# Layer 1's attention scores: from two products of 512 columns in two row groups to four of 256 columns in four row groups

## The chip, the cores and the metric

One Trainium2 chip; the kernel runs on 1 of its cores. The metric is the device time of one execution in microseconds (us), the median of several executions. The engines are TensorE (in the profile PE for its products and PEld for its weight loads), VectorE (DVE), ScalarE (ACT), GpSimd (POOL) and SyncE (SP, which here only issues transfers). Products are written to PSUM[...].

## The reference

Eight batches of 128 tokens of width 512 pass through four layers. Each layer is a cross-attention and then a feed-forward part, both added to the running `x`, which is normalised before each part:

```python
x = x + _L0_xattn_ref(_layernorm(x), ...)   # 32 heads of 128
x = x + _L0_ffn_ref(_layernorm(x), ...)     # base product and gated low-rank experts
x = x + _L1_xattn_ref(_layernorm(x), ctx_4096, mask, ...)
x = x + _L1_ffn_ref(_layernorm(x), ...)     # int8 product
x = x + _L2_xattn_ref(...)                  # 32 query heads, 8 key heads, rotary
x = x + _L2_ffn_ref(...)                    # weights rounded to NF4 and back
x = x + _L3_xattn_ref(...)
x = x + _L3_ffn_ref(...)
```

The change touches the attention of layer 1 only:

```python
def _L1_xattn_ref(qk, v, masks, Wq, bq, Wk, bk, Wv, bv, Wo, bo):
    W, H, D, DK = 128, 8, 128, 64
    # each batch's 128 x 512 is cut into 4 patches of 128 x 128
    q = einsum('ed,bdw->bew', Wq, qp) + bq[:, None]      # 64 rows: 8 heads of 8
    k = einsum('ed,bdw->bew', Wk, qp) + bk[:, None]
    val = einsum('ed,bdw->bew', Wv, vp) + bv[:, None]
    scores = einsum('bhdi,bhdj->bhij', qh, kh) / sqrt(8)
    scores = where(mask > 0, scores, -1e9)
    attn = softmax(scores)
    o = einsum('bhij,bhdj->bhdi', attn, vh)
    o = gelu(o)
    out = (einsum('de,bew->bdw', Wo, o) + bo[:, None]) * masks
```

A head has only 8 rows. For one patch of one batch there are eight score matrices of 128 x 128.

## The kernel before

All tensors are float32 unless a line says otherwise. The work is one long, unrolled program. Its backbone is a list of 128 units: a unit is one attention head for one half of the batches (four batches), first of layer 0 (`Unit0`, 64 units) and then of layer 2 (`Unit2`, 64 units). A unit projects keys and queries, makes scores three units ahead or two, turns the softmax's output through DRAM, weighs the values (L297), and every fourth unit adds a group's output to `x` (L218).

Everything shorter is put into *slots* between a unit's pieces. `slot()` calls what a table has written for the current slot number, and then works off some pieces of the NF4 rounding of layer 2's feed-forward weights. `short_stages(hf)` fills that table for one half: the feed-forward part of layer 0 (`F0`), layer 1's attention (`L1`), layer 1's feed-forward part (`F1`). So layer 1's attention for batches 0 to 3 runs while `Unit0` units of the second half are the main work, and for batches 4 to 7 while `Unit2` units of the first half are.

Within `L1`, batch i of a half starts at slot t = 18 + 13 i. `norm` runs at t - 1 and `project` at t: one product (L516) gives queries on partitions 0 to 63 and keys on 64 to 127, ScalarE adds the bias (L518) into `qk`, and VectorE makes four masked copies of the keys (L521) in `km`, in each of which only the rows of two of the eight heads are not zero. The 64 rows of keys are two strips of 32, and each strip holds four heads; so one product of a strip of queries with that strip's four masked copies gives the scores of four heads side by side. `score(b, n)` runs at t + 2, 5, 8 and 11, one patch each time: two products of 32 rows and 512 columns (L540) into two PSUM tiles; VectorE reads each, scales it and adds the mask (L542), then takes the maximum (L544); ScalarE takes the exponentials (L213); the result is scaled (L548), transposed in blocks (L240) and sent through DRAM by POOL's queue (L242, L245). `project_values` runs at t + 7 (product L527, read by VectorE at L529). `weigh(b, n)` runs at t + 9, 12, 15 and 18 (product L557 in four column groups, read by ScalarE at L558), `close` and `output` at t + 18 and t + 19. Where the batches' ranges overlap, a slot has a `score` of one batch and then a `weigh` of the one before: slots 33, 36, 46, 49, 59 and 62.

PSUM tiles come from two streams. The main stream has two banks for products, and one each for turns (`tp`), scores and weighed values; the units' own work uses it. The side stream rotates three banks for everything in the slots:

```python
main = Main("m", None, ps, {"mm": ("mm", 2), "tp": ("tp", 1), "sc": ("sc", 1), "pv": ("pv", 1)})
side = Stream("s", sub_pool("side", 2), ps, {k: ("side", 3) for k in ("mm", "tp", "sc", "pv", "po")})
```

So a new side tile waits until the one taken three tiles earlier has been read. Main's `tp` bank serves the first three units and the loading of the first contexts; after that a unit's turn goes through DRAM and main takes no `tp` tile while the side stream runs.

The framework that builds the program draws all waits itself. It also sets the order of each engine's instructions ahead of time, from the order of the calls and its own estimate of when each is ready.

Of the kernel before, what the change touches and what calls it, by code (L numbers as in the profile page):

```python
# [11 lines left out]
F32 = mybir.dt.float32  # L12
# [5 lines left out]
AF = mybir.ActivationFunctionType  # L18
ALU = mybir.AluOpType
# [4 lines left out]
P = 128  # L24
B = 8
D = 512
# [36 lines left out]
def kernel(ctx: ExitStack, tc: tile.TileContext, a, out):  # L63
    nc = tc.nc
    V, S, G, T = nc.vector, nc.scalar, nc.gpsimd, nc.tensor
# [15 lines left out]
    class Stream:  # L81


        def __init__(self, name, sb, ps, banks):
            self.name, self.sb, self.ps, self.banks = name, sb, ps, banks
# [46 lines left out]
    def along(v, n):  # L132

        return v.unsqueeze(2).to_broadcast([v.shape[0], v.shape[1], n])

    def times(v, n):

        return v.unsqueeze(1).to_broadcast([v.shape[0], n, v.shape[1]])
# [70 lines left out]
    def exps(dst, src, su, n, negm, scale=None):  # L209

        for h in range(n):
            by = 1.0 if scale is None else scale[:, h:h + 1]
            S.activation(dst(h), src(h), AF.Exp, bias=negm[:, h:h + 1], scale=by, accum_out=su[:, h:h + 1])  # L213
# [19 lines left out]
    def blocks_turned(pool_, src, name, bufs, queue=nc.sync):  # L233

        h, n = src.shape[1], src.shape[2] // P
        tb = pool_.tile([P, 4 * n, h, 32], F32, tag="tb" + name, name="tb", bufs=bufs[0])
        V.transpose(tb, src.rearrange("p h (c k) -> p c h k", k=32))  # L240
        far = dram.tile([4, 32, n, 4, 32 * h], F32, tag="far" + name, name="far", bufs=4)
        queue.dma_start(far.rearrange("a i s b n -> (a i) (s b n)"), tb.rearrange("p c h j -> p (c h j)"))  # L242
        pt = pool_.tile([P, n, 4, h, 32], F32, tag="pt" + name, name="pt", bufs=bufs[1])
        for b in range(4):
            queue.dma_start(pt[32 * b:32 * b + 32].rearrange("p s a h j -> p s a (h j)"), far[:, :, :, b, :].rearrange("a i s n -> i s a n"))  # L245
        return pt

    def project(st, w, xT):

        mm = st.mm()  # L250
        for c in range(DC):
            T.matmul(mm, lhsT=w[:, c, :], rhs=xT[:, c, :], start=c == 0, stop=c == DC - 1)  # L252
        return mm
# [90 lines left out]
    class Unit0(Unit):  # L344
        def project_k(self):
            st, g, grp = self.st, self.g, self.group
            if self.h == 0:
                grp.bias = ap_.tile([P, 4, P], F32, tag="rot", name="bias")
                load(grp.bias, a["l0_bias"][g])
            self.k = tile_of("k", 3)  # L350
            S.copy(self.k, project(st, of_head(a["l0_wk"][g], self.h), ctxT[:, :, self.hf * 512:(self.hf + 1) * 512]))

        def project_q(self):
            st, g, grp = self.st, self.g, self.group
            self.q = tile_of("q", 3)
            S.copy(self.q, project(st, of_head(a["l0_wq"][g], self.h), xT0[self.hf]))
            if self.h == 0:
                self.load_values()
            if self.h == 3:
                grp.wo = by_chunk(a["l0_wo"][g])  # L360
# [8 lines left out]
        def score(self):  # L369
            s = self.score_tile()  # L370
            mark[0] = V.tensor_add(s, self.scores(self.k), times(self.group.bias[:, self.h, :], HALF))
            V.tensor_add(s, s, neg0[:, self.hf * HALF:(self.hf + 1) * HALF, :])
            self.softmax(s)
            V.tensor_mul(self.su, self.su, anyv[:, self.hf * HALF:(self.hf + 1) * HALF])
            V.tensor_mul(s, s, along(self.su, P))
# [99 lines left out]

    class L1:
        def __init__(self, st, hf):
            self.st, self.hf = st, hf  # L480
# [33 lines left out]
        def project(self, b):  # L514
            mm = self.st.mm()
            T.matmul(mm, lhsT=self.wqk[:, 0:2, :].rearrange("p s d -> p (s d)"), rhs=self.h, start=True, stop=True)  # L516
            self.qk = self.l1.tile([P, D], F32, tag="qk1", name="qk1", bufs=1)
            S.activation(self.qk, mm, AF.Identity, bias=self.bqk)  # L518
            self.km = self.l1.tile([64, 4, D], F32, tag="km", name="km", bufs=1)
            for hd in range(4):  # L520
                V.tensor_scalar(self.km[:, hd, :], self.qk[64:128, :], self.h4[64:128, hd:hd + 1], None, ALU.mult)  # L521

        def project_values(self, b):
            mm = self.st.mm()
# [9 lines left out]
        def score(self, b, n):  # L534
            st, w = self.st, slice(n * P, (n + 1) * P)
            s = self.l1.tile([P, 8, P], F32, tag="s1", name="s1", bufs=1)
            scs = [st.sc() for j in range(2)]
            for j in range(2):
                r = slice(32 * j, 32 * (j + 1))
                T.matmul(scs[j], lhsT=self.qk[r, w], rhs=self.km[r, :, w], start=True, stop=True)  # L540
            for j in range(2):
                V.scalar_tensor_tensor(s[:, 4 * j:4 * j + 4, :], scs[j], 1.0 / math.sqrt(8.0), times(self.neg[:, w], 4), ALU.mult, ALU.add)  # L542
            mx = st.small(8, "mx")
            V.tensor_reduce(mx, s, AX.X, ALU.max, negate=True)  # L544
            su = st.small(8, "su8")
            exps(lambda h: s[:, h, :], lambda h: s[:, h, :], su, 8, mx)
            V.reciprocal(su, su)
            V.tensor_mul(s, s, along(su, P))  # L548
            self.pts[n] = blocks_turned(self.l1, s, "1", (1, 2), G)[:, 0]
# [115 lines left out]
    class Unit2(Unit):  # L665
# [20 lines left out]
        def project_q(self):  # L686
            self.q = tile_of("q", 3)
            rope(self.q, project(self.st, of_head(a["l2_wq"][self.g], self.h), xT2[self.hf]), cs[self.hf])
            if self.h == 3:
                self.group.wo = by_chunk(a["l2_wo"][self.g])  # L690
# [411 lines left out]
    with ExitStack() as early:  # L1102
        def sub_pool(name, bufs, **kw):
            return early.enter_context(tc.tile_pool(name=name, bufs=bufs, **kw))
# [10 lines left out]
        main = Main("m", None, ps, {"mm": ("mm", 2), "tp": ("tp", 1), "sc": ("sc", 1), "pv": ("pv", 1)})  # L1115
        side = Stream("s", sub_pool("side", 2), ps, {k: ("side", 3) for k in ("mm", "tp", "sc", "pv", "po")})


        NF4_PACE = ((2.1, 2.1), (0.9, 2.2), (0.2, 1.6), (1.6, 1.6))
        xT0, xT2 = [], []  # L1120
# [343 lines left out]
def build(arrays):  # L1464
    import concourse.bacc as bacc

    nc = bacc.Bacc("TRN2", target_bir_lowering=False, num_devices=1)
    aps = {
        n: nc.dram_tensor(f"in_{n}", v.shape, mybir.dt.from_np(v.dtype), kind="ExternalInput").ap()
        for n, v in arrays.items()  # L1470
    }
    out = nc.dram_tensor("out_0", (B, P, D), F32, kind="ExternalOutput").ap()
    with tile.TileContext(nc) as tc:
        kernel(tc, aps, out)
    return nc
# [9 lines left out]
```

## Time and profile before

| what | us |
|---|---|
| median of 3 executions | 3075.28 (3073.91 to 3076.26) |
| the profiled execution's own time | 3075.35 |
| span of its records | 3073.6 |
| TensorE products in flight | 3041.6 |
| VectorE busy | 1876.2 |
| ScalarE busy | 1373.3 |
| POOL busy | 384.4 |

The span is 1.75 us shorter than the time of the same execution. A row of a line's group gives count, then shortest, median and longest duration in ns, then first and last start. A row of the timeline gives start and duration in us, engine, line, operation, the tiles written and read, the shape, how many neighbours were merged, and in brackets how long the engine had been idle and what released it. A float32 product shows as two records, each of which is a pass over all its columns; a record's duration is from its start until its last result is out, so neighbours overlap: full-height passes of 512 columns start 0.429 us apart and last 0.59. "PE busy" therefore means that a product is in flight. Transfers keep the 16 DMA engines under half busy (37.3% for the largest queue).

### The profile page before, as it was taken

The page shows a single profiled execution, that of the slowest core. Times are in us where ns is not written, and L with a number is a line of the kernel's source. Part 1 is how long each engine was busy: PE and PEld are TensorE (multiplying, and loading weights), DVE is VectorE, ACT ScalarE, POOL GpSimd, SP SyncE. Part 2 cuts the span into 40 slices and gives each one's busy share as a digit, 9 for nine tenths or more (in the row PEclk, how much of TensorE's full clock was granted, in tenths as well). Part 3 has the DMA queues.
Part 4 walks back from the last instruction along what each step waited for, and adds up shares of the span by engine and source line. Part 5 has one row for each costly group of instructions (what it writes and reads, how often), then busy time and mean ns, then how long its engine had stood idle before and what let it go on. Part 6 is the DMA issues. An engine that isn't in the chain of part 4 may idle for free.

```text
span 3073.6 us, 35109 instructions
## 1 busy us (share of the span) xinstructions
PE 3041.6 (99%) x10720; PEld 1668.8 (54%) x10724; DVE 1876.2 (61%) x3765; ACT 1373.3 (45%) x3856; POOL 384.4 (13%) x490
## 2 busy tenths in 40 slices
PE   9999999999999999999999999999999999999999
PEld 4555555544444565555555554445656656555554
DVE  5666666657766566898889862214554555555544
ACT  4555555435654433665556641003343433433332
POOL 2000000101211021332111110001111111111110
PEclk9999999999999999999999999999999999999999
DMA  6434343336654533665344342223565645655540
GB/s 216 127 113 120 120 134 116 110 100 181 177 157 126 153 111 92 179 188 171 117 139 129 122 121 77 78 73 117 165 193 165 193 161 176 189 173 168 175 126 14
DMA packets 425564, 427.42 MB, mean 139 GB/s; under 512 B 40160, under 2 KB 315296, under 8 KB 424864
## 3 DMA queue, kind: packets, MB, share of 16 engines
q1 hardware_dynamic: 391200, 348.60, 37.3%
q10 hardware_dynamic: 23040, 41.95, 4.4%
q0 software_dynamic: 11136, 34.61, 3.8%
q8 instruction: 87, 1.43, 0.2%
q14 instruction: 101, 0.83, 0.1%
HBM read 308.70 MB, written 116.33 MB: 138 GB/s over the span
## 4 chain that ended last, share of the span: by engine, by line
PE 47%; DVE 3%; ACT 1%; issue 0%; POOL 0%; DVEq 0%; ACTq 0%; POOLq 0%
PE po L218 7%; PE tp L945 7%; PE mm L968 7%; PE mm L903 5%; PE mm L218 4%; PE pv L1028 4%; PE sc L1005 3%; PE mm L252 3%; PE mm L912 2%; PE mm L1096 1%; PE mm L1084 1%; PE pv L297 1%; DVE dq L750 1%; PE sc L280 1%; PE mm L682 1%; PE mm L672 1%
## 5 line engine op out<-in xcount | busy, mean ns | idle before, releaser
L252 PE MATMUL mm<-xT,w 128*128 128x512 f32 x1024 | 466.0, 597 | 2.3 <-DVE rot L662 2.3
L218 PE MATMUL mm<-w,o 128*128 128x512 f32 x1024 | 465.1, 598 | 1.6 <-ACT o L299 1.5
L739 ACT ACTIVATE ind<-nw,bounds 128x512 f32<-128x512 f32 (+2 forms) x510 | 350.0, 703 | 235.5 <-DVE dq L750 162.8
L750 DVE SCALAR_TENSOR_TENSOR dq<-ind,dq 128x512 f32<-128x512 f32 (+2 forms) x476 | 333.1, 700 | 23.0 <-ACT ind L739 8.2
L252 PEld LDWEIGHTS mm<-xT,w 128*128 128x128 f32 x1024 | 190.1, 191 | 220.5 <-issue 211.7
L218 PEld LDWEIGHTS mm<-w,o 128*128 128x128 f32 x1024 | 189.7, 191 | 220.4 <-issue 208.5
L213 ACT ACTIVATE s<-s,nm 128x128 f32<-128x128 f32 x512 | 198.3, 388 | 101.9 <-DVE nm L271 101.2
L968 PE MATMUL mm<-w,xT 128*128 128x512 f32 x512 | 233.9, 592 | 0.0
L218 PE MATMUL po<-w,o 128*128 128x512 f32 x512 | 233.2, 594 | 0.0
L252 PE MATMUL mm<-ctxT,w 128*128 128x512 f32 x512 | 230.4, 593 | 0.8 <-ACT ctxT L1249 0.8
L384 PE MATMUL mm<-w,ctxT 128*128 128x512 f32 x512 | 230.4, 593 | 0.0
L213 ACT ACTIVATE p<-sc,nm,rq 128x256 f32<-128x256 f32 x256 | 141.1, 562 | 114.6 <-DVE nm L1010 110.9
L219 DVE TENSOR_TENSOR x<-x,mm 128x512 f32<-128x512 f32 x128 | 87.1, 680 | 143.1 <-PE mm L218 142.8
L280 PEld LDWEIGHTS sc<-k,q 128*128 128x128 f32 x1024 | 131.7, 192 | 49.8 <-issue 44.6
L159 POOL TENSOR_TENSOR rs<-rs,mhalf 128x1 f32<-128x1 f32 x64 | 38.2, 598 | 950.6 <-DVE rs L180 510.0
L218 PEld LDWEIGHTS po<-w,o 128*128 128x128 f32 x512 | 96.3, 190 | 110.6 <-issue 102.8
L384 PEld LDWEIGHTS mm<-w,ctxT 128*128 128x128 f32 x512 | 94.7, 190 | 108.0 <-issue 107.1
L903 PE MATMUL mm<-xT,w 128*128 128x512 f32 (+1 forms) x352 | 152.5, 592 | 0.8 <-DVE x L219 0.8
L299 ACT COPY o<-pv 128x512 f32<-128x512 f32 x128 | 74.3, 580 | 173.8 <-PE pv L297 173.7
L1009 DVE TENSOR_REDUCE nm<-sc 128x2 f32<-128x512 f32 x128 | 85.3, 674 | 103.1 <-PE sc L1005 102.8
L252 PEld LDWEIGHTS mm<-ctxT,w 128*128 128x128 f32 x512 | 93.4, 190 | 99.1 <-issue 97.8
L968 PEld LDWEIGHTS mm<-w,xT 128*128 128x128 f32 x512 | 97.0, 190 | 89.4 <-issue 84.7
(254 smaller groups left out, 4749.0 us busy)
## 6 DMA issues: line engine op xcount, KB each, us to landing
w<-in_l_wq SPq DMA_DIRECT2D x128, 256.0 KB
w<-in_l_wo SPq DMA_DIRECT2D x128, 256.0 KB
far<-tb SPq DMA_DIRECT2D x125, 256.0 KB
pt<-far SPq DMA_DIRECT2D x500, 64.0 KB
far<-tb SPq DMA_DIRECT2D x60, 512.0 KB
pt<-far SPq DMA_DIRECT2D x240, 128.0 KB
far<-tb SPq DMA_DIRECT2D x63, 384.0 KB
pt<-far SPq DMA_DIRECT2D x252, 96.0 KB
```

Source lines behind the costliest of these rows:

```text
L213: S.activation(dst(h), src(h), AF.Exp, bias=negm[:, h:h + 1], scale=by, accum_out=su[:, h:h + 1])
L218: T.matmul(mm, lhsT=o(h), rhs=wo[h], start=h == 0, stop=h == 3)
L252: T.matmul(mm, lhsT=w[:, c, :], rhs=xT[:, c, :], start=c == 0, stop=c == DC - 1)
L280: T.matmul(sc[:, i, :], lhsT=self.q[:, i * P:(i + 1) * P], rhs=k[:, i * P:(i + 1) * P], start=True, stop=True)
L384: T.matmul(mm, lhsT=ctxT[:, c, toks(self.hf * HALF + i)], rhs=grp.wv[c], start=c == 0, stop=c == DC - 1)
L739: S.activation(ind, w, AF.Relu, bias=bounds[:n, i:i + 1], scale=(down + up)[i][1])
L750: V.scalar_tensor_tensor(dst, ind, step, dst, ALU.min, ALU.subtract if i == len(down) else ALU.add)
L903: T.matmul(mm[:n, :], lhsT=w[c][:, j * P:j * P + n], rhs=xT[:, c, :], start=c == 0, stop=c == DC - 1)
L945: T.matmul(it.kv[:, s, :], lhsT=lhsT, rhs=it.wkv[c // 2][:, c % 2, :], start=c == 0, stop=c == DC - 1)
L968: T.matmul(mq, lhsT=self.xT[it.hf][:, c, cols(it.b)], rhs=it.wq[c], start=c == 0, stop=c == DC - 1)
L1005: T.matmul(sc[:, i, :], lhsT=it.qT[2 * j + i], rhs=it.kT, start=True, stop=True)
L1028: T.matmul(pv, lhsT=it.v[:, j, :], rhs=it.pts[j], start=j == 0, stop=j == 1)
```

## The change

`project` keeps a second copy of the queries on partitions 64 to 127 (`again`, made by ScalarE), and `km` holds the four masked key copies as two on partitions 0 to 63 and two on 64 to 127. `score` makes four products of 32 rows and 256 columns, each in a row group of its own (partitions 0, 32, 64, 96), each into a PSUM tile of its own. Three of these come from the side stream's three banks, the fourth from the bank of main's `tp`. VectorE reads each of the four with an instruction of its own, and the pairs of heads go to the places they had before.

```diff
@@ project
-            self.qk = self.l1.tile([P, D], F32, tag="qk1", name="qk1", bufs=1)
-            S.activation(self.qk, mm, AF.Identity, bias=self.bqk)
-            self.km = self.l1.tile([64, 4, D], F32, tag="km", name="km", bufs=1)
+            qk = self.l1.tile([P, D], F32, tag="qk1", name="qk1", bufs=1)
+            S.activation(qk, mm, AF.Identity, bias=self.bqk)
+            again = self.l1.tile([P, D], F32, tag="q1", name="q1", bufs=1)
+            S.copy(again[64:128, :], qk[0:64, :])
+            self.q = [qk, qk, again, again]
+            self.km = self.l1.tile([P, 2, D], F32, tag="km", name="km", bufs=1)
             for hd in range(4):
-                V.tensor_scalar(self.km[:, hd, :], self.qk[64:128, :], self.h4[64:128, hd:hd + 1], None, ALU.mult)
+                r = 64 * (hd // 2)
+                V.tensor_scalar(self.km[r:r + 64, hd % 2, :], qk[64:128, :], self.h4[64:128, hd:hd + 1], None, ALU.mult)
@@ score
-            scs = [st.sc() for j in range(2)]
-            for j in range(2):
+            scs = [st.psum(kind, (P, 2, P)) for kind in ("sc", "sc", "sc", "sc4")]
+            for j, sc in enumerate(scs):
                 r = slice(32 * j, 32 * (j + 1))
-                T.matmul(scs[j], lhsT=self.qk[r, w], rhs=self.km[r, :, w], start=True, stop=True)
-            for j in range(2):
-                V.scalar_tensor_tensor(s[:, 4 * j:4 * j + 4, :], scs[j], 1.0 / math.sqrt(8.0), times(self.neg[:, w], 4), ALU.mult, ALU.add)
+                T.matmul(sc, lhsT=self.q[j][r, w], rhs=self.km[r, :, w], start=True, stop=True)
+            for sc, h in zip(scs, (0, 4, 2, 6)):
+                V.scalar_tensor_tensor(s[:, h:h + 2, :], sc, 1.0 / math.sqrt(8.0), times(self.neg[:, w], 2), ALU.mult, ALU.add)
@@ the streams
         side = Stream("s", sub_pool("side", 2), ps, {k: ("side", 3) for k in ("mm", "tp", "sc", "pv", "po")})
+
+        side.banks["sc4"] = ("tp", 1)
```

## The prediction

> **What bounds the kernel now.** I read the page's busy times first, then the stretches of layer 1, the lines of its scores, and two short timelines around single scores.
>
> The page, rows of the whole execution:
>
> ```profile
> span 3073.6 us, 35109 instructions
> PE 3041.6 (99%) x10720; PEld 1668.8 (54%) x10724; DVE 1876.2 (61%) x3765; ACT 1373.3 (45%) x3856; POOL 384.4 (13%) x490
> ```
>
> TensorE is busy or has a product in flight all the time, so time taken off it should come off the end, unless a wait takes its place. Busy times of the two stretches in which layer 1's scores run (first and second half of the batches; columns PE, PEld, DVE, ACT, POOL, then granted clock):
>
> ```profile
> 667.00:878.00 211.00, 211.00 (x843) 102.40 (x843) 161.57 (x278) 122.53 (x415) 40.10 (x72) 1.00 0.60 169
> 1199.00:1406.00 207.00, 198.81 (x950) 107.38 (x950) 183.76 (x292) 125.55 (x491) 66.54 (x92) 0.98 0.58 172
> ```
>
> They differ. In the first TensorE never idles and VectorE has slack (162 of 211 us). In the second VectorE is at 184 of 207 us and TensorE already loses 8 us. What the score products and their readers cost, from the two lines' own rows:
>
> ```profile
> L540 PE MATMUL sc<-km,qk x128: 587/625/692, 667.0 to 1394.6; 32*128 32x512 f32 x128
> L542 DVE SCALAR_TENSOR_TENSOR s<-sc,neg x64: 646/681/693, 668.6 to 1405.5; 128x512 f32<-128x512 f32 x64
> ```
>
> 128 records are 64 products, two records each: 32 scores of two products. One score of the first half, in order of time (start, duration, engine):
>
> ```profile
> 723.90 1.13 PE L540 MATMUL sc<-km,qk 32*128 32x512 f32 x4
> 724.96 0.64 PE L557 MATMUL pv<-pt,vt 128*32 128x128 f32 x16
> 725.06 1.29 DVE L542 SCALAR_TENSOR_TENSOR s<-sc,neg 128x512 f32<-128x512 f32 x2 [3.43 <-PE sc L540]
> ```
>
> Four records in 1.13 us, where four of a full-height 512-column product stand 0.43 us apart: the two row groups already run side by side. And the `weigh` product (L557) starts 1.06 us after the score, before VectorE has touched the score: it has a bank of its own. In the second half the reader comes late:
>
> ```profile
> 1224.37 1.00 PE L527 MATMUL mm<-wqk,h 128*128 128x64 f32 x8
> 1225.30 1.43 PE L540 MATMUL sc<-km,qk 32*128 32x512 f32 x4
> 1226.66 4.56 PE L218 MATMUL mm<-w,o 128*128 128x512 f32 x10
> ...
> 1234.10 0.28 DVE L529 TENSOR_TENSOR vt<-mm,bv 128x128 f32<-128x128 f32 x1
> ...
> 1236.09 1.27 DVE L542 SCALAR_TENSOR_TENSOR s<-sc,neg 128x512 f32<-128x512 f32 x2
> ```
>
> The value projection (L527) is read at last at 1234.10, the score of 1225.30 from 1236.09. VectorE trails by some 9 us here, and only free banks let TensorE go on.
>
> **The products: a gain of 13.2 us.** Between neighbouring records (single instructions of the timeline) a score's first pass starts at 723.899, the second at 724.432 (0.533 later), the next work at 724.956 (0.525 later). Full-height records stand 0.429 apart, so 0.427 of each is the stream of 512 columns and about 0.1 is loading and changing the array's shape. With 256 columns the stream halves to 0.2135: 0.320 + 0.312, and two more row groups start 0.0066 later each, as the two do now: 0.645 instead of 1.058 us. 0.413 x 32 scores = 13.2 us of TensorE, if four row groups run at once as two do. Near row: L557 runs four column groups with starts 0.006 apart, 16 records in 0.57 us. Bounds: nothing saved if the groups go two by two; no more than 13.2.
>
> **VectorE: +4.5 to +9.5 us, partly hidden.** Two reads of 128x512 (681 ns) become four of 128x256. The row for that width is L837, SBUF to SBUF, 418 ns: 4 x 0.418 - 2 x 0.681 = 0.31 us a score, 9.9 in all; back to back they overlap (starts 0.604 apart for 0.69), which makes it 0.14, or 4.5. I take 4.5. In the first half the slack covers it; in the second, half of it (2 us) can reach TensorE. Without cover it is the whole 4.5 to 9.9. The key masks (L521, 486 ns, four a batch) stay as many on as many partitions: nothing.
>
> **ScalarE: +4.6 us, hidden.** One copy of 64x512 a batch, 8 x 0.57 (copies of that width, L351 and L356). It runs behind L518 beside VectorE's four masks (1.7 us), and the batch's first score comes 6 us or more after L518; ScalarE is busy 123 and 126 us in the two stretches. Behind it wait the exponentials, by 0.57 us eight times. If nothing covered it: 4.6. No DMA is added or moved, so the queues of SP and POOL get nothing; POOL issues the turned scores when VectorE has them, later by the 0.14.
>
> **The banks: +4 and +4 us, the doubtful part.** The side stream rotates three banks. A score took two, now it takes all three, and the unused turn bank of the main stream. Two waits are new.
>
> First, `weigh` in the same slot as a score, 12 of 32 times (slots 33, 36, 46, 49, 59, 62 of each half), had the third bank; now it needs the score's first bank, free when the first quarter is read. Score end (0.72) + 0.41 of reading + about 0.09 of semaphores = 1.22 us after the score's start, where TensorE is ready at 0.645: 0.58 us each with VectorE at hand. VectorE's lag at these twelve, by the readers' starts: 0.03, 0.49, 0.03, 0.03, 0.19, 0.03 in the first half; 0, 1.35, 0.56, 1.10, 0.81, 1.99 in the second. Taken in order that is 7.0 for the twelve and 6.2 of lags: 13.2 us, all of the gain. But the framework orders each engine ahead of time by readiness (L297 of this unit stands at 1231.06, behind the outputs written after it), so it can put a main product between. Then a lone `weigh` costs 0.20 more: score and `weigh` together take 1.83 us out of the stream, apart 1.255 + 0.772. That is 2.4 for twelve. Between 2.4 and 13.2 I take 4, as in the first half the reader is nearly always at hand.
>
> Second, a score that follows a value projection needs that projection's bank. In the first half VectorE has read it in time. In the second, three scores (1225.30, 1282.86, 1386.30) would wait for 1234.38, 1287.88 and 1389.90: 9 + 5 + 3.6 = 17.6 us if nothing is put between. The outputs (L218, 4.6 us right behind the first) and other products can be, and an earlier stall lets VectorE catch up, so later ones (2.5 and 1.3 us before L540 already) shrink. Between 0 and 17.6 I take 4.
>
> Queued behind a waiting score on TensorE is all of the main attention work, and VectorE and ScalarE behind that.
>
> **A rule against the change.** The row: a score's readers need 1.29 us now and 1.43 after, its products 1.06 now and 0.645 after. The Trainium skill's "TensorEngine Tiling (Array Packing)", section "PSUM Bottleneck", says in substance that tiling quickens TensorE and not the emptying of PSUM, which can become the limit; "Gotcha 1: PSUM Pressure" adds that row tiles need different banks. By the rule alone each bank is held at VectorE's pace, the in-order price stands (13.2 + 17.6), and the sum is +18. By the trace the reader is at hand in the first half and there is other work for TensorE, and the sum is negative. No run here shows four row groups. I go by the trace for the first half and between the two for the second.
>
> **Sum.** -13.2 + 4 + 4 = -5.2, the 2 us of VectorE being inside the second 4. The profiled execution took 3075.35 us (span 3073.6 and 1.75 around it), 0.07 from the median 3075.28: 3075.35 - 5.2 = 3070.
>
> **Rivals.**
> - *Nearly all kept.* The ordering fills every wait; only the 2.4 for lone `weigh`s is paid: -10.8, 3064.5. For: no idle TensorE in the first half. Against: in the second, stalls at L540 (2.5 and 1.3 us) show an order that did not foresee VectorE.
> - *The banks decide: slower.* In the second half scores and `weigh`s wait for VectorE in the written order: 17.6 + 9.3 there, less 6.6 of gain, some 5 of relief and 5 of the first half's net gain: about +10, 3085. Place: L540 and L557 from 1199 to 1406. It decides once the waits exceed 13.2 us, 0.9 us for each of the fifteen products named. For: lags of 4 to 10 us there. Against: the planner's reordering seen above.
> - *No fourfold row groups.* The products go two by two: no gain, the 8 of waits stay, and each pair's own loading (0.1 x 2 x 32 = 6) is paid: +14, 3089. Against: four column groups do run together.
>
> **How the numbers follow.** Forecast (3065 to 3076) 0.36, nearly all kept 0.24, banks decide 0.34, no fourfold groups 0.06. 0.2% is 6.15 us, about what a measurement of this kernel can tell from no change. Faster (under 3069.1): 0.15 of the forecast and 0.23 of the second, 0.38. Slower (over 3081.4): 0.26 of the banks, 0.05 of the last, and 0.01 of reordering far behind the change: 0.32. The same: 0.30. The range runs from 3061 (nearly all kept, a little relief on top) to 3090 (the two slower cases); the likeliest case alone is 3065 to 3076.
>
> **What would show it.** The score's group: 256 records of 32x256, eight in 0.65 to 0.75 us for each score; over 1.0 and the fourfold groups fail. VectorE's reads x128 near 0.41 us. `weigh` moved away from the score by one main product, or TensorE idle before L557 on a releaser L542. Idle TensorE before L540 between 1199 and 1406: up to 6 us more and the forecast stands, over 15 us and the slower rival. First half shorter by 4 to 6 us; the second unchanged within 4. Wrong altogether if the stages with no score move by more than 5 us.

## The result, and the profile after

| | before | after |
|---|---|---|
| median of the compared runs, us | 3075.24 (3073.87 to 3077.42, 22 runs) | 3079.12 (3075.93 to 3083.83, 22 runs) |
| ratio | | 1.0014, 95% interval 1.0008 to 1.0020 |
| the profiled execution's own time, us | 3075.35 | 3079.07 |

The change costs 3.9 us, or 0.13%. The interval leaves out no change, and the forecast was on the other side of it (3070.0, a gain of 5.2).

The page of after, rows of the whole execution. Compare TensorE's row with the one before: 5.8 us less in flight, and 3.7 us more span.

```profile
span 3077.3 us, 35445 instructions
PE 3035.8 (99%) x10852; PEld 1670.8 (54%) x10852; DVE 1883.5 (61%) x3829; ACT 1377.4 (45%) x3864; POOL 382.7 (12%) x490
```

The two stretches with layer 1's scores (PE, PEld, DVE, ACT, POOL, then granted clock). TensorE, which never idled in the first, is now 3.5 us short of it; in the second it lies 14 us short instead of 8.

```profile
667.00:878.00 211.00, 207.48 (x900) 102.98 (x898) 165.50 (x310) 125.56 (x425) 41.01 (x73) 1.00 0.60 171
1199.00:1406.00 207.00, 193.06 (x985) 106.14 (x984) 183.72 (x314) 125.22 (x490) 63.81 (x91) 0.99 0.57 169
```

The lines of the scores and of their readers (L546 and L548 are L540 and L542 of before):

```profile
L546 PE MATMUL sc<-km,qk x128: 374/412/479, 665.9 to 1398.4; 32*128 32x256 f32 x128
...
L546 PE MATMUL sc<-km,q x128: 374/412/479, 666.0 to 1398.5; 32*128 32x256 f32 x128
...
L548 DVE SCALAR_TENSOR_TENSOR s<-sc,neg x128: 381/414/426, 666.7 to 1408.9; 128x256 f32<-128x256 f32 x128
```

256 records of 256 columns, as forecast, and readers of 0.414 us each.

**A score of the first half** (TensorE's timeline; then VectorE's, same stretch; L563 is `weigh`, L557 before):

```profile
722.07 0.48 PE L546 MATMUL sc<-km,qk 32*128 32x256 f32 x2
722.08 0.48 PE L546 MATMUL sc<-km,q 32*128 32x256 f32 x2
722.39 0.38 PE L546 MATMUL sc<-km,qk 32*128 32x256 f32 x2
722.40 0.38 PE L546 MATMUL sc<-km,q 32*128 32x256 f32 x2
723.28 0.65 PE L563 MATMUL pv<-pt,vt 128*32 128x128 f32 x16 [0.50 <-DVE s L548]
```

```profile
722.80 1.42 DVE L548 SCALAR_TENSOR_TENSOR s<-sc,neg 128x256 f32<-128x256 f32 x4 [3.43 <-PE sc L546]
```

The four row groups run at once: first passes at 722.07 and 722.08, second passes at 722.39 and 722.40. A score with main work behind it takes 0.64 to 0.65 us to the next start. Here `weigh` follows, and it starts 1.21 us after the score instead of 0.65: its bank (the piece of PSUM that one side tile takes) is the one that VectorE's first read has just left.

**The waits.** TensorE, 667 to 878: what it waited for, us in total, times, longest. Before, this view has no line.

```profile
PE pv L563 <- DVE s L548: 3.0, 6, 0.5
PE tp L793 <- DVE s L548: 0.5, 1, 0.5
```

And in the second half, 1195 to 1450, the three largest of after:

```profile
PE sc L546 <- DVE vt L535: 4.3, 3, 2.2
PE pv L563 <- DVE s L548: 3.7, 5, 1.3
PE sc L546 <- DVE km L527: 3.3, 5, 2.4
```

against the four of before that come first:

```profile
PE pv L297 <- DMA pt<-far: 2.5, 1, 2.5
PE sc L540 <- ACT s L700: 2.5, 1, 2.5
PE sc L540 <- DVE km L521: 1.3, 1, 1.3
PE sc L540 <- DVE s L542: 0.6, 1, 0.6
```

L535 is VectorE's read of the value projection, L527 the key masks. A score now waits for the bank of the value projection, a `weigh` for that of the score.

The waits for key masks did not grow. By the times, before's 2.5 us put down to ScalarE is one too: VectorE's last mask ends at 1258.27, and the score follows 0.14 us later, before the last of ScalarE's four records has ended. So masks cost 3.8 us before and 3.3 after.

```profile
1257.38 0.89 DVE L521 TENSOR_SCALAR km<-qk,h 64x512 f32<-64x512 f32 x2
1258.41 1.13 PE L540 MATMUL sc<-km,qk 32*128 32x512 f32 x4 [2.45 <-ACT s L700]
```

**Scores that are torn.** The score of 1225.30 before, with its surroundings, after (TensorE; then VectorE):

```profile
1222.99 0.48 PE L546 MATMUL sc<-km,qk 32*128 32x256 f32 x2
1223.03 0.48 PE L546 MATMUL sc<-km,q 32*128 32x256 f32 x1
...
1223.66 4.56 PE L218 MATMUL mm<-w,o 128*128 128x512 f32 x10
1228.05 1.09 PE L297 MATMUL pv<-pt,v 128*128 128x128 f32 x8
1228.98 1.02 PE L218 MATMUL mm<-w,o 128*128 128x512 f32 x2
1232.21 0.67 PE L546 MATMUL sc<-km,q 32*128 32x256 f32 x2 [2.20 <-DVE vt L535]
1232.80 1.98 PE L218 MATMUL mm<-w,o 128*128 128x512 f32 x4
```

```profile
1228.05 0.28 DVE L535 TENSOR_TENSOR vt<-mm,bv 128x128 f32<-128x128 f32 x1
...
1228.91 2.95 DVE L554 TENSOR_TENSOR s<-s,su 128x1024 f32<-128x1024 f32 x1
1231.78 0.28 DVE L535 TENSOR_TENSOR vt<-mm,bv 128x128 f32<-128x128 f32 x1
```

The order made ahead of time put three of the four products at 1222.99 and the fourth, whose bank the value projection holds, nine microseconds later. It waits 2.20 us there all the same, since VectorE has a 2.95 us product of another score between the projection's two reads. And the lone product then takes 0.59 us by itself (1232.21 to 1232.80); in a group it would have cost next to nothing (whole groups of three take 0.637 us in three_products below, of four 0.644 here). That score takes 0.67 + 0.59 us of TensorE, twice a whole one. It was split before too, its second row group 0.3 us behind, and took 1.36 us (1225.30 to 1226.66). Before, two scores of the second half are split so (1.36 and 1.65 us); the other 14 take 1.06.

The 2.95 us product is itself a late one: the same instruction takes 1.22 us in all 16 scores of the first half. In the second half six take 1.5 to 2.95, and these six are the ones that run beside GpSimd's rotary product (L669, 1.28 us, here at 1229.49), which the stretch of the first half does not have. Before, five of seven such are longer. It makes VectorE late in both kernels; no run here takes it away.

A second kind of tearing, at 1256, comes from the key masks, of which VectorE writes the last ones at 1255.46 to 1256.87:

```profile
1256.09 0.70 PE L546 MATMUL sc<-km,qk 32*128 32x256 f32 x4 [2.40 <-DVE km L527]
1257.01 0.70 PE L546 MATMUL sc<-km,q 32*128 32x256 f32 x4 [0.22 <-DVE km L527]
1257.64 1.43 PE L218 MATMUL mm<-w,o 128*128 128x512 f32 x2
```

1.55 us instead of 0.645. Of the second half's 16 scores 9 run whole. Three run as two pairs (1256.09, 1312.71, 1365.07); they are the first scores of their batches, and the masks of the second pair are done 0.9 us after those of the first. Four are the third scores of their batches, next to the value projection. Three of these are split 3 + 1 (from 1222.99, 1282.98 and 1390.27), and the lone product waits for that projection's bank; one goes into four lone products of 0.62 us (from 1335.73), with the value projection and an output projection between them, which hold a side bank each. Waits aside, the three cost 2.1 us more than whole scores, the four 3.6; 0.9 was lost in before by its two split ones.

**The account.** TensorE's time between the same main products of before and after, from one profiled execution each. Idle is time with nothing in flight; the rest is split by whose slot it is (from a product's start to the next start, less idle).

| us, after less before | total | idle | scores | `weigh` | other products |
|---|---|---|---|---|---|
| first half (662 to 948 of before) | -2.6 | +3.4 | -6.1 | 0 | +0.1 |
| between the halves (948 to 1021) | +1.5 | +0.2 | 0 | 0 | +1.2 |
| second half (1198 to 1451) | +5.4 | +5.9 | -1.8 | +0.3 | +1.0 |

(The first half's -6.1 holds 0.5 us of results still coming out ahead of a waiting `weigh`; the products themselves give 16 x 0.413 = 6.6.) Outside these three the two executions differ by 0.6 us just after them and by nothing more, apart from their starts, where after gains 1.05 us.

### The profile page after: what moved, and what is told of

It reads as the page before. It is cut to its first block, busy times and chain, and to the rows that moved or that the text cites. A ratio compares the mean times of both kernels' runs of the same rounds, so it can differ in the third digit from the quotient of the medians.

```text
span 3077.3 us, 35445 instructions
## 1 busy us (share of the span) xinstructions
PE 3035.8 (99%) x10852; PEld 1670.8 (54%) x10852; DVE 1883.5 (61%) x3829; ACT 1377.4 (45%) x3864; POOL 382.7 (12%) x490
## 4 chain that ended last, share of the span: by engine, by line
PE 47%; DVE 3%; ACT 1%; issue 0%; POOL 0%; DVEq 0%; ACTq 0%; POOLq 0%
PE po L218 7%; PE tp L951 7%; PE mm L974 7%; PE mm L909 5%; PE mm L218 4%; PE pv L1034 4%; PE sc L1011 3%; PE mm L252 3%; PE mm L918 2%; PE mm L1102 1%; PE mm L1090 1%; PE pv L297 1%; DVE dq L756 1%; PE sc L280 1%; PE mm L688 1%; PE mm L678 1%
```

## The experiments

Each time below is a median, against the median of before taken along with it on the same chip; the ratio with its 95% interval is that of the runs, and can differ a little from the quotient of the two medians.

**One bank fewer, and the same products in other banks.** The first kernel leaves out the fourth product (its read takes the third tile again), which in the fourfold group takes next to no time of its own, and so leaves one of the side stream's banks free. The second has the same three products, all in side banks.

```diff
-            scs = [st.psum(kind, (P, 2, P)) for kind in ("sc", "sc", "sc", "sc4")]
+            scs = [st.psum(kind, (P, 2, P)) for kind in ("sc", "sc", "sc4")]   # three_products
+            scs = [st.psum(kind, (P, 2, P)) for kind in ("sc", "sc", "sc")]    # three_side_banks
...
-            for sc, h in zip(scs, (0, 4, 2, 6)):
+            for sc, h in zip(scs + scs[2:], (0, 4, 2, 6)):
```

> The changed kernel with three of the four products: heads 6 and 7 of layer 1 are left without scores of their own (their read takes the tile of heads 2 and 3 again). Four reads, the second copy of the queries and the row groups stay; one of the three side banks stays free, so weigh has a bank of its own as before. Theory A (the gain of the products, 13 us, is eaten by waits for side banks that VectorE has not read yet): 3062 to 3067 us, weigh 0.65 us after the score with no wait. Theory B (the extra reads on VectorE and the copy on ScalarE eat it): 3074 to 3080. Theory C (the new order of instructions as a whole is worse): 3074 to 3080, with losses spread outside layer 1.

> As three_products (heads 6 and 7 of layer 1 left without scores of their own), but the three tiles come from the three side banks, and main's turn bank stays unused: only the banks differ from three_products, which took 3069.2 us. Theory A (what the changed kernel lost is the wait for side banks): 3076 to 3080 us, weigh again 1.2 us behind the score in the first half. Theory B (the reads on VectorE are the loss): 3068 to 3071.

Measured: 3069.20 against 3075.56, 0.9979 (0.9972 to 0.9986), and 3079.91 against 3075.36, 1.0016 (1.0010 to 1.0023). The same products and the same reads; the third side bank alone costs 10.7 us, and with it the sign changes. The place where it starts, three_products first, then three_side_banks (TensorE's timeline, same score):

```profile
721.16 0.48 PE L546 MATMUL sc<-km,qk 32*128 32x256 f32 x2
...
721.79 0.64 PE L563 MATMUL pv<-pt,vt 128*32 128x128 f32 x16
```

```profile
723.93 0.48 PE L546 MATMUL sc<-km,qk 32*128 32x256 f32 x2
...
725.14 0.65 PE L563 MATMUL pv<-pt,vt 128*32 128x128 f32 x16 [0.50 <-DVE s L548]
```

0.63 us from score to `weigh`, against 1.21. In its profiled execution three_products keeps all of the products' gain in the first half (-6.9 us to before, no waits), and three_side_banks 2.8 of it, as after does. In the second half three_products stands at +0.4 at 1451 of before (the order of the main products differs there: -1.9 at 1445, +0.8 at 1469). Its scores take 3.1 us less, not 6.6: 6 of the 16 are torn although a side bank is free, three first scores, one third and two fourth ones. A first score waits for a mask with its last product:

```profile
1250.56 0.67 PE L546 MATMUL sc<-km,q 32*128 32x256 f32 x2 [1.56 <-DVE km L527]
```

The profiled execution of three_side_banks is 5.6 us under its median, so its second half (+3.1) is not taken as typical. After is no slower than three_side_banks (3.9 and 4.6 us over before), so the fourth group and main's `tp` bank have no cost that these medians resolve.

**VectorE's four reads by themselves**, on the kernel before, in both halves and in one of them:

```diff
-            for j in range(2):
-                V.scalar_tensor_tensor(s[:, 4 * j:4 * j + 4, :], scs[j], ..., times(self.neg[:, w], 4), ...)
+            for h in (0, 4, 2, 6):
+                V.scalar_tensor_tensor(s[:, h:h + 2, :], scs[h // 4][:, h % 4:h % 4 + 2, :], ..., times(self.neg[:, w], 2), ...)
```

> The kernel before with each of its two score tiles read by VectorE in two instructions of 256 columns in place of one of 512: 128 reads instead of 64, products and banks as before. Theory A: VectorE's extra 4.5 us hardly matter, 3075 to 3077 us. Theory B: they are the loss, 3079 to 3085. Theory C: unclear, the order shifts a little.

> The kernel before with doubled reads for batches 0 to 3 only. If VectorE's time costs only where it is nearly full: 3074.5 to 3076.5 us. If it costs in both halves alike: 3077 to 3079.

> As four_reads (which took 3080.5 us), with the doubled reads for batches 4 to 7 only. Theory B2 (extra time on VectorE costs in the second half only, where VectorE is nearly full, and costs more than its own 2.2 us because TensorE's clock is halved for 3.4 us after a stall): 3079 to 3082. If VectorE's reads cost the same everywhere: 3077.5 to 3078.5. If four_reads was only an accident of its order: 3074 to 3077.

Measured: both 3080.52 against 3075.56, 1.0017 (1.0011 to 1.0024); first half alone 3075.64 against 3075.63, 1.0000 (0.9992 to 1.0008); second alone 3078.42 against 3075.36, 1.0012 (1.0005 to 1.0019). So the reads cost 5.0 us (3.4 to 7.4 by the interval), none of it resolved in the first half and 3.1 (1.5 to 5.8) in the second. In the second, TensorE's waits of four_reads are led by

```profile
PE sc L540 <- DVE km L521: 7.2, 3, 4.2
```

which was 1.3 us before, or 3.8 with the wait above: VectorE comes later to the key masks. VectorE's own added time in the second half is some 2 us (1.42 instead of 1.29 us for 16 scores). It reaches the end in full; whether as more than its size, as the medians have it, the intervals leave open.

**The change in the first half only**, and then with `weigh` in main's bank for weighed values:

```diff
+            if self.hf == 0:        # the change, as in after
...
+            else:                   # two products and two reads, as before
...
-            pv = self.st.pv()                                              # first_half_weigh_main, in weigh
+            pv = self.st.pv() if self.hf else self.st.psum("pvm", (P, 4, P))
+        side.banks["pvm"] = ("pv", 1)
```

> The change for batches 0 to 3 alone, the old scores for batches 4 to 7. The traces of before and after put a gain of 2.6 us into the first half (of which 1.5 goes again while the rotary rows are fetched near 1000 us) and a loss of 5.4 into the second. Theory A: the two halves are independent, 3072 to 3074.5 us. Theory B: the same sign, as VectorE is the busy engine in the second half only, 3070 to 3074. Theory C: no sum of halves, anything from 3072 to 3080.

> The change for batches 0 to 3 only, with their weigh in the main stream's bank; old scores and banks for batches 4 to 7. The first half should gain all of 6.6 us, less what the fetch of rotary rows near 980 us gives back: 3069 to 3072. If gains of the first half are lost whatever the second does: 3074 to 3077.

Measured: 3075.59 against 3075.56, 1.0001 (0.9993 to 1.0009); 3074.16 against 3075.63, 0.9998 (0.9989 to 1.0006). Both traces are shorter by 2.7 and 3.3 us at the end of the first half, lose 2.6 and 2.4 again between the halves, and the first another 3.5 in the second half, where its TensorE order is that of before (its profiled execution is 2.9 us over its median). Neither the gain nor its loss can be told from nothing in the medians. Where it went between the halves (TensorE's waits, 960 to 1000; L675 turns the rotary rows of layer 2, L654 before):

```profile
PE tp L675 <- issue: 6.4, 1, 6.4
```

against 4.5 us before. In this execution an earlier arrival waits longer. That is no rule: in three_groups and groups_first_half below, which gain 3.2 us and more ahead of it, the wait is 3.0 and 3.4 us.

**Filling that wait.** Four products of 512 columns, whose result is not used, in slot t + 2 of the first half, on before and on the best variant below:

```diff
+                def filler():
+                    idle = side.mm()
+                    for i in range(4):
+                        T.matmul(idle, lhsT=ctxT[:, 0, 0:P], rhs=ctxT[:, 0, 0:512], start=True, stop=True)
+
+                put(t + 2, filler)
```

> The kernel before with four idle-filling products of 512 columns (their result is not used) in slot t+2 of the first half of layer 1, ahead of the turns of the rotary rows, where TensorE waited 4.5 us at L654 and then ran at half the clock for 3.4 us. They cost TensorE about 1.7 us of their own. If the wait is set by a chain outside TensorE, it shrinks, the halved clock at about 980 us is gone, and the time is 3072 to 3074.5. If the rotary chain follows TensorE's own work, the wait stays at 4.5 us behind the added products, and the time is 3077 to 3080.

> groups_first_half (three row groups in the first half only, 3072.5) with the same four idle-filling products. If they fill the wait at the rotary rows: 3069 to 3071.5. If the wait only moves behind them: 3074 to 3077.

Measured: 3073.61 against 3074.80, 0.9998 (0.9990 to 1.0006), and 3073.84 against 3074.80, 0.9995 (0.9987 to 1.0003). The stretch 960 to 1010 of before, of before_filler and of after (columns as in the two stretches above, the granted clock after POOL):

```profile
960.00:1010.00 50.00, 45.50 (x151) 23.46 (x150) 21.62 (x55) 21.45 (x55) 8.31 (x9) 0.97 0.41 119
```

```profile
960.00:1010.00 50.00, 48.63 (x161) 24.82 (x161) 21.14 (x53) 21.43 (x55) 8.72 (x9) 1.00 0.44 130
```

```profile
960.00:1010.00 50.00, 45.22 (x144) 23.45 (x143) 19.18 (x51) 21.30 (x55) 8.33 (x9) 0.93 0.41 125
```

The wait shrinks from 4.5 to 1.4 us under the filler, so it is set from outside TensorE, and the granted clock stays at 1.00, which saves one stretch of 3.4 us at half the clock. The four products take 3.4 us, not the 1.7 expected, since each is two passes of 0.43. So 3.1 + 1.7 - 3.4 = 1.4 us are gained there, as the execution shows. The medians do not resolve it, and on the best variant it gains nothing: the wait is down to 0.4 us there, but that execution has a halved clock four times in the second half, the one without filler once.

**Removing the waits one by one.** On after: `weigh` in main's bank in both halves; `weigh`, `close` and `output` one slot later, so that none follows a score; the values projected one slot earlier; the masks made one slot earlier. On before: the masks one slot earlier; and the second tile read by ScalarE instead of VectorE, which leaves the mask out there.

```diff
+        side.banks["pv"] = ("pv", 1)                        # weigh_main_bank
-                    call(t + 9 + 3 * n, "l1", "weigh", b, n)
+                    call(t + 10 + 3 * n, "l1", "weigh", b, n)     # weigh_later; close, output at t + 19, t + 20
-                call(t + 7, "l1", "project_values", b)
+                call(t + 6, "l1", "project_values", b)      # values_early
-                call(t - 1, "l1", "norm", b)
-                call(t, "l1", "project", b)
+                e = 1 if i else 0                           # masks_early, after_masks_early
+                call(t - 1 - e, "l1", "norm", b)
+                call(t - e, "l1", "project", b)
+            S.activation(s[:, 4:8, :], scs[1], AF.Copy, scale=1.0 / math.sqrt(8.0))   # scalar_read
```

> The changed kernel with layer 1's weigh in the main stream's bank for weighed values, so that it no longer needs a bank that the score just before it has taken. If weigh carries most of the banks' cost: 3069 to 3073 us, and weigh 0.65 us behind a score in the first half. If the scores' own wait for three banks (behind value projections) carries it: 3076 to 3080.

> The changed kernel with weigh, close and output of layer 1 one slot later, so that no slot has a score and a weigh right behind it. Theory A: the 0.57 us at each of six pairs in the first half (3.4 us) come back, and a part of the second half's, while a weigh by itself costs 0.2 more: 3070 to 3075 us, no wait of 1.21 us between a score's start and the next product. Theory B and C: 3077 to 3081.

> The changed kernel with the value projection of layer 1 at the sixth slot of a batch instead of the seventh, so that a slot lies between it and the next score. Theory A for the second half: the scores' waits for the projection's bank (4.3 us in the trace) go, and fewer scores are split into parts that no longer run side by side (four were, some 0.8 us for each extra part): 3073 to 3077 us. If those waits only move to the next product: 3078 to 3081.

> The kernel before with norm and project of layer 1 one slot earlier for the second to fourth batch of each half, so that the key masks have three slots instead of two before the batch's first score. Theory B3 (time on VectorE costs only where TensorE waits for the key masks, at 1258, 1313 and 1364 us[...]): the waits of 2.5 and 1.3 us and the halved clock behind them go, 3069 to 3073 us. If the second half is full of VectorE's work as such: 3074 to 3077.

> The changed kernel with the same shift. Theory B3: 3.3 us of waits for masks and a window of halved clock go, 3073 to 3077 us; the waits for banks stay. If VectorE as such binds the second half: 3078 to 3081.

> The kernel before with the second of a score's two tiles read by ScalarE in place of VectorE, and without adding the mask there (the mask is left out for heads 4 to 7). Takes 0.6 us a score off VectorE, 9.7 in each half, and puts 0.7 on ScalarE; products and banks as before. Theory B2: the second half gets shorter by 4 to 9 us, 3066 to 3072. If VectorE does not bound the second half: 3074 to 3077.

| kernel | us | before | ratio (95%) |
|---|---|---|---|
| weigh_main_bank | 3075.66 | 3075.63 | 1.0002 (0.9994 to 1.0010) |
| weigh_later | 3079.23 | 3075.56 | 1.0012 (1.0004 to 1.0020) |
| values_early | 3080.47 | 3075.57 | 1.0016 (1.0010 to 1.0023) |
| masks_early | 3078.18 | 3075.57 | 1.0010 (1.0001 to 1.0018) |
| after_masks_early | 3080.67 | 3075.57 | 1.0015 (1.0008 to 1.0021) |
| scalar_read | 3076.89 | 3075.36 | 1.0007 (0.9999 to 1.0015) |

Only the bank gives something back: 3.5 us (3079.12 to 3075.66) of the 10.7. In its trace the first half gains only 0.7 of that, as `weigh` now shares main's one bank with the units and 2.3 us of idle remain there of 3.4; the second half stands at +1.4 instead of +5.4. The moves in time fail. The waits of weigh_later in 667 to 878 are the one for the turn and a new one of 0.3, so its aim was met; in 1195 to 1450 its largest are

```profile
PE pv L563 <- DVE s L548: 4.2, 3, 1.6
PE sc L546 <- DVE km L527: 3.9, 5, 1.8
```

and those of values_early, which has no wait for the value projection any more,

```profile
PE sc L546 <- DVE km L527: 5.1, 4, 1.9
PE pv L563 <- DVE s L548: 4.9, 7, 1.4
```

In values_early the wait that was removed comes back at other lines (4.3 us gone, 3.9 more at these two and L533). And scalar_read, which takes VectorE from 184 to 176 us in that stretch, is not faster than before:

```profile
1199.00:1406.00 207.00, 197.21 (x943) 107.57 (x942) 175.88 (x279) 131.72 (x501) 67.31 (x92) 0.98 0.59 171
```

So VectorE's busy time alone is not what sets the pace there; its order may be (the 2.95 us product ahead of a 0.28 us read), or what stretches that product, or the exponentials, to which ScalarE adds its reads in scalar_read. That is argued; these were not told apart.

**Fewer columns with the old banks' number.** 384 columns in each of two row groups, in two side banks, and the two heads left over in a third row group, two products of 128 columns into main's `tp` bank; three reads. Then the same in the first half only, and with the earlier masks.

```diff
+            for hd in range(3):
+                V.tensor_scalar(km[0:64, hd, :], qk[64:128, :], self.h4[64:128, hd:hd + 1], None, ALU.mult)
...
+            scs = [st.psum(kind, (P, n, P)) for kind, n in (("sc", 3), ("sc", 3), ("sc4", 2))]
...
+            for j, q in enumerate((self.km[64:96, 2, w], self.q1[64:96, w])):
+                T.matmul(scs[2][:, j, :], lhsT=q, rhs=self.km[64:96, j, w], start=True, stop=True)
```

> A version of the whole computation with three row groups: two products of 384 columns into two side banks, and in the third group two of 128 (heads 3 and 7) into main's turn bank; three reads, and ScalarE makes the copies and masks for the third group, so that VectorE has three masks a batch instead of four. By the trace of the products a pass of 384 columns streams 0.32 us, so a score should take 0.85 us instead of 1.06, and weigh keeps a bank of its own. Theory A with B2: -6.7 for the products, +1 for the third read, -2 for the masks: 3066 to 3071 us. If the small products of the third group do not run beside the others: 3075 to 3079.

> three_groups for batches 0 to 3 only. By its trace the first half gains 3.2 us and the second loses 2.1: 3071 to 3073.5 us. If the second half's loss in three_groups was chance: 3073 to 3076.

> three_groups (three row groups, whole computation, 3072.4 us) with the same shift: gains that do not touch each other, 3066 to 3070 us. If it gains nothing on top of three_groups: 3071 to 3074.

Measured: 3072.36 against 3075.36, 0.9994 (0.9985 to 1.0002); 3072.47 against 3075.63, 0.9990 (0.9983 to 0.9996); 3072.91 against 3075.57, 0.9991 (0.9983 to 0.9999). A score of three_groups, with nothing waiting:

```profile
666.12 0.59 PE L545 MATMUL sc<-km,qk 32*128 32x384 f32 x2
666.13 0.48 PE L547 MATMUL sc<-km 32*128 32x128 f32 x2
...
666.54 0.49 PE L545 MATMUL sc<-km,qk 32*128 32x384 f32 x2
...
666.96 3.27 PE L252 MATMUL mm<-xT,w 128*128 128x512 f32 x7
```

0.84 us, 0.21 under before, 16 times 3.4 us in each half. The first half gives 3.2 to 3.4 in all three traces. The second gives nothing: the medians with and without it are 3.0 and 3.2 us under before. groups_first_half, at -3.2 us, is the best of the variants that compute everything; its interval (0.9983 to 0.9996) just leaves out no change from before.

## Why the prediction was wrong

**The sum, by experiment.** With a side bank left free, products, reads and copy stand 6.4 us under before (three_products); the forecast's -13.2 and the reads' 2 would be -11.2. The third side bank then costs 10.7 us; the forecast had 6 for it (4 + 4, less the reads' 2). -6.4 + 10.7 = +4.3 is near the +3.9 measured. So two steps failed, by some 5 us each: every score was counted as whole, and the banks were priced too low. The first sets the size of the gain, the second turns its sign.

**The products: -13.2 forecast, about -8.4 found.** The size of a whole score was right to the hundredth: 0.645 forecast, 0.64 to 0.65 measured, four row groups at once. The failed step is "0.413 x 32": the forecast multiplied by all 32 scores, as if each ran whole. In the first half all 16 do (-6.6). In the second 7 of 16 are torn, and the scores' slots shrink by 1.8 us. That is 4.8 of the 6.0 us by which the second half missed its forecast. A group runs whole only if all its banks and masks are ready at one moment, and whatever is late splits it: the masks at three first scores (2.1 us), the side banks of projections at four third scores (3.6), against 0.9 lost before. Two lone products (1.2 us) take more than a whole score did before (1.06). This was not among the rivals. A free bank alone does not cure it: in three_products one third score is torn instead of four, but two fourth ones are, and 3.1 us are gained there instead of 1.8. What part VectorE's added reads and the order made ahead of time have in this, no run tells apart.

**The banks: 4 + 4 forecast, 10.7 for the third side bank.** The 10.7 hold its waits, what it adds to the tearing, and what follows from both. The two terms of the forecast, in the traces:
- `weigh` in the same slot. The in-order price was right: 1.22 us after the score forecast, 1.21 measured. (The twelve lags listed add up to 6.6; 6.2 is what stands above the usual 0.03.) "The framework can put a main product between" holds in one half only: in the first the written order was kept in all six cases, in the second none of the six follows its score directly. With one turn of the NF4 rows behind a score as a seventh, that is 3.5 us of idle in the first half, where the forecast had about 2. In the second half `weigh` waits 3.7 us in all for the score's bank, behind other products.
- A score after a value projection. 4 forecast between 0 and 17.6, 4.3 us of waits measured. Here the order was changed, as foreseen, but by tearing the score.

All idle time of the second half grew by 5.9 us, with about 6 forecast. That is close partly by luck: the forecast put 2 of it down to VectorE's reads, and no wait of after can be assigned to them.

**VectorE's reads: "half of it (2 us) can reach TensorE" forecast, inside the second 4; 5.0 measured alone.** The split between the halves was right (0.0 in the first). The size was too low: on the kernel before, the reads lengthen the waits for the masks from 3.8 to 7.2 us. In after those waits are 3.3 us, so there the reads' time must be in the later release of banks, or in the tearing; that was not separated.

**ScalarE's copy: 4.6 forecast and taken as hidden.** The first half closes without it: -6.6 and about +4.0 are the measured -2.6. In the second it ends at 1254.75, 1308.66 and 1361.30, 1.3 us or more before the first scores above, although one score comes only 5.1 us after the bias (L518 of before), not the "6 us or more" of the forecast. It was not run alone.

**The sum, by the traces.** First half: -6.6 and 2 forecast, -2.6 measured. Second: about -0.6 forecast, +5.4. Between the halves: nothing forecast, +1.5, a stretch that moved from -3.2 to +2.6 us over the kernels here.

**The rivals.** "The banks decide" had the direction, the place and the two lines. Its size was 17.6 + 9.3 of waits in the second half; TensorE's idle there grew by 5.9. The rule against the change had the direction too; its +18 is the price in the written order, which only the first half kept. "No fourfold row groups" is excluded by the records.

**The marks.** Waits before the score's line went from 4.4 us (three lines) to 7.6, which is within "up to 6 more: the forecast stands", and yet the second half lost: a mark on idle time cannot see products that are busy in pieces. The other two told the failure: the first half got 2.6 us shorter (4 to 6 asked), the second 5.4 longer (within 4 asked). The stages with no score moved by 1.5 us at most, as asked.

## What to carry to other kernels

A packed group of products is worth its gain only while it stays whole, so count the banks and operands that have to be ready at the same moment, and not only those that exist. Do not multiply a saving over a stretch where the engine already waits for others. Where it is never short of work the saving is made in full, but even that can be lost later: of three kernels that saved 2.7 to 3.3 us in the first half alone, the medians kept 0.0, 1.5 and 3.2. Where a reader engine trails, its added time reaches the end: measure it by doing that part alone, in each half.

## What the hardware showed

- The granted clock of TensorE is halved in pieces of 3.413 us or twice that, which begin on one grid of 3.413 us: in before at 980.06, 1259.95 and 1314.56 us, which are 82 and 16 pieces apart. Between 40 and 3060 us there are these three in before, three in after (975, of 6.8 us, 1258 and 1463), and none in before_filler. Each piece of 3.4 us costs about 1.7 (half of it, an estimate). The idle times ahead of them were 1.3 to 4.8 us long; others of 1.3 to 2.7 us were not followed by one. The Trainium skill's "TensorE: Matmul & The Clock Gate", Part 1, gives the same window and calls it free-running, with an idle window of about 3.4 us as the condition; here less than that was enough (1.33 us ahead of 1314.56). Such pieces come and stay away between runs of one kernel: of the 25 runs of before taken beside the fillers, the seven with a mean granted clock of 0.997 took 3075.6 to 3077.5 us, the six with 0.999 took 3070.5 to 3074.6.
- A lone product of 32 rows and 256 columns takes 0.59 to 0.62 us of TensorE, four in four row groups 0.645, two pairs one after the other 1.55 with 0.22 of waiting in it.
- A score's first pass takes 0.533 us to the next with 512 columns and 0.320 with 256. So 256 columns are 0.213 us, and 0.107 do not depend on the columns; what these are made of, no run shows.
